# One bound register for 1323 indirect gathers, in place of one register move each

## The chip, the cores and the metric

The kernel runs on one core of a Trainium2 chip, as one launch. The metric is the device time of a run in microseconds (us); the table below gives the median of three runs. The profile shown is of one further execution, taken by the hardware profiler.

## The reference

Two relational graph attention layers over a graph of 3125 nodes with 768 features and 53125 edges, then a residual and a layer norm. The edges come sorted by destination; each has one of three relations. Cut to what matters:

```
def rgat_conv(x, W, q, k, b, src, dst, etype, heads, out_ch, n_nodes):
    xr = einsum('nd,rdf->rnf', x, W)          # 3 x 3125 rows of 768
    oi, oj = xr[etype, dst], xr[etype, src]   # gathered by edge
    alpha = leaky_relu(oi @ q + oj @ k, 0.2)
    m = segment_max(alpha, dst)
    e = exp(alpha - m[dst])
    z = segment_sum(e, dst)
    a = e / (z[dst] + 1e-16)
    msg = a[:, :, None] * oj.reshape(-1, heads, out_ch)
    return segment_sum(msg, dst) + b

h = elu(rgat_conv(x, W1, q1, k1, b1, ..., heads=4, out_ch=192))
h = rgat_conv(h, W2, q2, k2, b2, ..., heads=1, out_ch=768)
out = layernorm(x + h)
```

All arithmetic is in float32.

## The kernel before, in words

Nodes are taken in 25 blocks of 128. The edges of a block lie in slots of 128 edges: 18 slots for each of 24 blocks and 9 for the last, 441 slots in all (`SL`, `SLL`, `NK`). A layer makes a table in DRAM with one row for each node and relation, 9600 rows (`NP * R`), which holds the node's features times that relation's weights and the attention's product for the source side. For every slot, one indirect DMA on GpSimd's queue then gathers 128 rows of a table, one to each partition, by the 128 row numbers of the slot.

There are three stages, and each gathers every slot once:

- Stage 1 (`phase1`) makes layer 1's table `ftab1` by dense products on TensorE (line 626, evicted by ScalarE on line 638). Beside it, it gathers the small rows of `kt1` (4 numbers an edge) into the buffers `kt`, and from them works out the softmax weights `pall` of layer 1 (`a_alpha`, line 560, is the first that reads the gathered numbers).
- Stage 2 (`phase2`) walks the slots: it gathers a row of 772 numbers an edge from `ftab1` into nine buffers `share`, splits each into a high and a low part (ScalarE line 785, VectorE line 799), makes a one-hot matrix `sel` of the destinations (line 787, on VectorE for every third slot and on GpSimd for the others), and adds the slot up with TensorE (line 818). Between them stand the dense products that make layer 2's table `ftab2` (line 873).
- Stage 3 (`phase3`) gathers rows of `ftab2` into six buffers `G` of six slots each, takes the softmax (line 1017 first reads the gathered numbers), adds the slots up (line 1090), and writes the layer norm's output.

The order of the instructions on each engine is written out by hand: a loop over slots (or over dense products in stage 1) calls the parts of the work at fixed distances, under `manual_schedule`. GpSimd runs its instructions in that order: in stages 1 and 3 nearly only gathers, in stage 2 gathers with the one-hot matrices of two slots in three between them. A gather may wait for a buffer to come free, and for an earlier gather's landing: eight semaphores (`DMASW0` to `DMASW7`) are used by the gathers in turn.

All gathers go through one helper, `gather_rows`. It passes `bounds_check=NP * R - 1`, the highest row that may be read. Row numbers of places past a block's own edges are set beyond it, so nothing is read for them; for four blocks, which are the first to fill their buffers, the row numbers are cut to the highest row (`rfirst`), so that every place is filled. The instruction takes the bound from a register of GpSimd. Given a plain number, it is lowered to two instructions: a register move, which stands right before the gather in GpSimd's program, and the gather.

A second kernel for edges that are not sorted as assumed stands behind a test at the end, and isn't executed with these inputs.

Of the kernel before, what the change touches and what calls it, by code (L numbers as in the profile page):

```python
# [18 lines left out]
DRAM = bass.MemoryType.DRAM  # L19
# [5 lines left out]
#: Masks an edge out of a maximum: a power of two, exact in bfloat16.  # L25
BIG = float(2**100)
#: Past every row of a layer's sums.
NOWHERE = 1 << 13
#: Slots per load of the destination rows.
# [7 lines left out]
#: Slots of 128 edges that a block of 128 nodes has on the fast path.  # L37
SL = 18
CAP = SL * P
#: And the last block, of fewer nodes.  # L40
SLL = 9
#: Entries before and behind the edges in their copies in DRAM.
FRONT = 256
BACK = CAP + 256
#: Rows gathered at once in the second layer, in slots.
PART = 6
#: Of so many slots there, those whose sums are float32 products.
# [4 lines left out]
def kernel(  # L52
# [9 lines left out]
    """The same for edges sorted by destination: at most CAP to a block of 128 nodes, 128 to a node.  # L62

    Returns a number that isn't 0 where the edges aren't so, and `out` then isn't to be used; every
    address stays in bounds for any edges.

    A block's edges start at `S[b]`, in SL slots of 128, and what is past its own edges counts for
    nothing. Rows come with (p * row) split into H + L, H of float32r's precision, so that two
    passes of one-hot matmuls add them up exactly as float32 would; dense products are HH + HL + LH.
    """  # L70
# [20 lines left out]
    OOB = float(1 << 20)  # L91

# [32 lines left out]
    def split3(to, q, work, shape):  # L125
        """q as a sum of three bfloat16."""
        c = work.tile(shape, F32, name="c3", bufs=2)
        V.tensor_copy(to[0], q)
        V.tensor_sub(c, q, to[0])
        V.tensor_copy(to[1], c)  # L130
        c2 = work.tile(shape, F32, name="c3", bufs=2)
        V.tensor_sub(c2, c, to[1])
        V.tensor_copy(to[2], c2)

    class Buffers:
        """What is loaded at first, in its order, each as soon as a buffer is free."""
# [32 lines left out]
    # ------------------------------------------------------------------ edges  # L169
    def prepare(work, bank, wide, half):  # L170
        """Copies of the edges' arrays for the slots, where the blocks start, and the flag; bit by bit."""
# [50 lines left out]
        # what is out of order, and nodes of more than 128 edges  # L222
# [26 lines left out]
    def transposes(psum, blocks):  # L249
        """The blocks turned, side by side: DT / 2 tiles of two parts."""  # L250
        pts = []
        for i in range(DT // 2):
            pt = psum.tile([P, 2, 2 * P], F32, name=f"pt{i}", bufs=2)
            for f in range(2):
                for c, a in enumerate(blocks):
                    T.transpose(pt[:, f, c * P:(c + 1) * P], a[:, (2 * i + f) * P:(2 * i + f + 1) * P], ident)
            pts.append(pt)
        return pts

    def split_parts(work, pts, w, name="t"):  # L260
        """The first w columns of each as H + L."""
        parts = []
        for i, pt in enumerate(pts):
            H, L = (work.tile([P, 2, w if name != "t" else 2 * P], F32R, name=f"{name}{s}{i}",
                              bufs=2 if name == "t" else 1) for s in "HL")
            S.copy(H[:, :, :w], pt[:, :, :w])
            V.tensor_sub(L[:, :, :w], pt[:, :, :w], H[:, :, :w].bitcast(F32))
            parts.append((H, L))
        return parts

    def times(to, a, parts):
        """a's products with what was split, added up."""
# [8 lines left out]
    # ------------------------------------------------------------------ attention of layer 1, early  # L281
    def weights_kq(buf, work, psum, bank, wk, kqs, wH, wL, nodes, more):
        """W1 split; W1[r] @ [k | q] split, and to the left of it zeros."""
# [53 lines left out]
    def nodes_kq(buf, pre, work, psum, bank, wk, kqs, wH, wL, qq, more, edges_ready):  # L337
        """The k products of all nodes, to DRAM, and the q; between them block 0's products with W1."""
        NCH = NB // 2 + 1

        def chunk(m):
            """Its first block, how many: at first block 0 alone."""
            return (2 * m - 1, min(2, NB + 1 - 2 * m)) if m else (0, 1)
# [37 lines left out]
        def first(i):  # L381
            """A third of a product of block 0 and half of W1[r]."""
# [31 lines left out]
        def begin(m):  # L414
            """Beside the weights' products: the first nodes."""
# [4 lines left out]
        # how many of block 0's thirds go beside which step  # L420
# [20 lines left out]
    def gather_rows(to, tab, b, j):  # L441
        """Past a block's edges nothing is read; a buffer's first rows are read whole."""
        i = ridx[:, b]
        if b in first_rows:
            i = rfirst[:, first_rows[b]]
        G.indirect_dma_start(out=to, out_offset=None, in_=tab, in_offset=_index(i[:, j:j + 1]),  # L446
                             bounds_check=NP * R - 1, oob_is_err=False)
# [6 lines left out]
    def at(t, rw, off, ap, s):  # L454
        """A view of an edge array in DRAM from edge s + off on."""
# [25 lines left out]
    def second_weights(r, wH, wL):  # L481
        """W2[r] in W1[r]'s place, with W2[r] @ [k | q] between its halves; piece by piece."""
# [9 lines left out]
    # ------------------------------------------------------------------ layer 1's tables and weights  # L492
    def phase1(pre, work, psum, wH, wL, qq):
# [103 lines left out]
        # buffers that are free by then  # L597
# [95 lines left out]
        # the last blocks' products go by W1[r], that W2[r] can take its place  # L693
# [4 lines left out]
        # what is done beside which product, by block  # L698
# [4 lines left out]
        for b in [*reversed(range(NB - 1)), NB - 1]:  # L703
            for d, f in steps if b < NB - 1 else last:
                # the first blocks' gathers are behind
# [35 lines left out]
    # ------------------------------------------------------------------ layer 1's sums, layer 2's table  # L741
    def phase2(work, psum, wH, wL):
# [11 lines left out]
        # the last block, of fewer slots, comes first  # L754
# [3 lines left out]
        def slot(k):  # L758
            """Block and slot of it."""
# [8 lines left out]
        def whole(k):  # L768
            """Of the first slots, with no dense products yet, every other's sums are float32 products."""
            return k < 8 and k % 2 == 1  # L770
# [92 lines left out]
        def d_part(b, r, c, i):  # L863
            """A third of a product of a block of h and half of W2[r]."""
# [70 lines left out]
    def x_load3(b):  # L935
        """x and layer 2's bias of a block, for the third phase."""
        nc.sync.dma_start(xbs[b % len(xbs)], xb_d[b * P:(b + 1) * P, :])

    # ------------------------------------------------------------------ layer 2's sums, residual, layer norm
    def phase3(work, psum):  # L940
# [24 lines left out]
        def a_local(b):  # L965
            """The slots' destinations, by slot; past 256 not exact, and none of the block's."""
# [5 lines left out]
        def a_spread(b, i):  # L972
            """Four slots' destinations to all partitions."""
# [76 lines left out]
        def whole(k):  # L1050
            """Slots whose sums are float32 products, to spare the split of their rows."""
            return k % 3 == 0 if late(k) else k * WHOLE[0] % WHOLE[1] < WHOLE[0]

        def late(k):
            """After the last gather."""
# [109 lines left out]
    with tc.manual_schedule():  # L1165
        with tc.tile_pool(name="share", bufs=1) as pool:
            share = [pool.tile([P, RW], F32, name=f"share{i}") for i in range(9)]
            # in the third phase: x and layer 2's bias, then the output
            two = pall.rearrange("p b j h -> p (b j h)")
            xbs = [t[:, :D] for t in share] + [two[:, i * D:(i + 1) * D] for i in range(2)]  # L1170
            with tc.tile_pool(name="wbuf", bufs=1) as wbuf:
                wH = wbuf.tile([P, R * DT, D + 2], F32R, name="wH")
                wL = wbuf.tile([P, R * DT, D + 2], F32R, name="wL")
                with tc.tile_pool(name="pre", bufs=1) as pre:
                    qq = pre.tile([P, NB, H1, R], F32, name="qq")
                    with tc.tile_pool(name="work0", bufs=1) as work, tc.tile_pool(
                        name="psum0", bufs=1, space=PSUM
                    ) as psum:
                        # products in one half, what they are turned into in the other
# [31 lines left out]
def kernel(  # L1211
# [9 lines left out]
    """Two relational graph attention layers, x + layers, layer norm.  # L1221

    Edges are first sorted by block of 128 destinations into slots of 128 edges, each slot of one
    block (`count_edges`, `place_edges`). A layer then makes a table of x @ W[r] with the attention's two products
    (`dense`), and walks the slots: it gathers the edges' rows, and keeps a running softmax of
    each block's 128 nodes (`edges`), as flash attention does, so that the destinations' degrees
    are free.
    """
# [11 lines left out]
    # A block of c edges has max(1, ceil(c / 128)) slots.  # L1240
# [43 lines left out]
    def attention_weights(ly, w, kq, work, psum):  # L1284
        """W[r] @ k behind the first half of W[r]'s columns, W[r] @ q behind the second."""
# [15 lines left out]
    def table_rows(ly, work):  # L1301
        """Buffers for rows of the table: per head its features and a one, then the heads' k products."""
# [7 lines left out]
    def dense(ly, block, w, rows, tab, qtab, work, psum, before=None):  # L1310
        """The table's rows and the q products of every node, block by block of nodes."""
# [42 lines left out]
    def count_edges(prep):  # L1354
        """What a slot needs of each edge (rows of the two tables, place in the block), and its rank."""
# [19 lines left out]
        # rank of each edge among its block's: first along a partition, then over partitions  # L1375
# [19 lines left out]
    def place_edges(prep, psum, erec, oh, s, cnt, below, ones):  # L1395
        """Edges to their slots; what is left of a slot leads nowhere."""
# [4 lines left out]
        # slots of each block, and the first of them  # L1401
# [10 lines left out]
        # an edge's place, in rows of rec_d: slot by slot within a partition  # L1412
# [23 lines left out]
        # a slot's block, and whether it is its block's first or last  # L1436
# [16 lines left out]
        # where a slot's block goes once it is whole; else nowhere  # L1453
# [22 lines left out]
    def edges(ly, tab, qtab, agg, work, psum):  # L1476
        """Each block's weighted sums of rows, and of the weights, by head: each slot adds its own to
        those so far, scaled to the maxima so far."""
# [21 lines left out]
        def scores(k):  # L1500
# [4 lines left out]
            # one where edge e leads to node n, by node and by edge; a penalty where it doesn't  # L1505
# [98 lines left out]
    def per_node(ly, n, a, plus, work):  # L1604
        """What a block's sums give: over the sum of the weights, plus `plus`."""
# [139 lines left out]
```

## Time and profile before

| | |
|---|---|
| median of 3 runs | 2310.36 us (2303.12 to 2312.99) |
| span of the profiled execution, first to last instruction | 2301.8 us |
| instructions in the span | 37988 |
| TensorE busy | 2053.6 us, 89% |
| TensorE weight loads busy | 1779.3 us, 77% |
| VectorE busy | 1636.5 us, 71% |
| ScalarE busy | 1232.2 us, 54% |
| GpSimd busy | 1751.5 us, 76%, 1684 instructions |
| gathers (line 446) | 1323, mean 1069 ns (`kt`), 1136 ns (`share`), 1161 ns (`G`) |
| register moves of line 446 | 1323, 29 ns each |
| moved by the DMA engines | 507.92 MB |

The profiled execution has no separate device time beside its span; the median of the runs is 8.6 us above the span.

How to read it: PE is TensorE, PEld its weight loads, DVE VectorE, ACT ScalarE, POOL GpSimd, SP the engine that issues most plain DMAs. A name with a q (POOLq) is the engine's sequencer, [...] its time is not counted as busy. [...] "out<-in" names the buffers, L446 is line 446, x378 a count. In a list of waits, the number triple is the total in us, how often, and the longest one; in brackets in a list in order of time stands how long the engine was idle before. "issue" is time in which the engine waited for nothing that the profile shows.

### The profile page before, as it was taken

What the parts mean: (1) busy time and instruction counts of PE and PEld (TensorE: products, weight loads), DVE (VectorE), ACT (ScalarE), POOL (GpSimd) and SP (SyncE); (2) the same over time, 40 slices, a digit from 0 to 9 for tenths busy, and PEclk for the clock granted to TensorE, in tenths of its full rate; (3) what the DMA queues carried; (4) which work ended last, traced back from release to release, by engine and by line L of the source; (5) the groups of instructions that cost most, each with busy time, mean ns of one, the idle gap of its engine ahead of it and who ended that gap; (6) DMA issues with size and microseconds to landing.
All of it is one profiled execution on the core that took longest, in us unless ns stands there. A gap on an engine that the chain in (4) does not pass through costs nothing.

```text
span 2301.8 us, 37988 instructions
## 1 busy us (share of the span) xinstructions
PE 2053.6 (89%) x11380; PEld 1779.3 (77%) x11380; DVE 1636.5 (71%) x4349; ACT 1232.2 (54%) x2745; POOL 1751.5 (76%) x1684
## 2 busy tenths in 40 slices
PE   6999988888985899999999999999499898898986
PEld 5888877888885899999999999998365555555554
DVE  7634434444433899999999999995387777777766
ACT  5411211111111788888888888884255554555553
POOL 4157777777776888888888888883777777777773
PEclk9989999999998899999999999999699999999998
DMA  6545444454455977777777777775888888888882
GB/s 181 171 135 177 163 150 143 161 168 145 158 193 168 316 243 230 233 228 240 235 231 237 236 235 234 234 230 186 292 287 285 284 293 278 289 261 285 274 268 73
DMA packets 153482, 507.92 MB, mean 221 GB/s; under 512 B 40362, under 2 KB 53697, under 8 KB 153269
## 3 DMA queue, kind: packets, MB, share of 16 engines
q0 software_dynamic: 85408, 333.97, 48.0%
q1 hardware_dynamic: 57631, 155.46, 18.8%
q10 hardware_dynamic: 10230, 15.98, 2.1%
q8 instruction: 94, 1.54, 0.3%
q14 instruction: 119, 0.97, 0.1%
HBM read 428.29 MB, written 93.81 MB: 227 GB/s over the span
## 4 chain that ended last, share of the span: by engine, by line
PE 39%; DMA 8%; POOL 8%; DVE 6%; issue 6%; ACT 2%; POOLq 0%; DVEq 0%; ACTq 0%
PE po L873 14%; PE acc L1090 13%; PE acc L818 10%; DMA G<-ftab,ridx 5%; POOL share L446 3%; POOL sel L787 2%; POOL G L446 2%; DVE L L799 2%; DVE L L1079 1%; DMA share<-ftab,ridx 1%; ACT H L785 1%; PE bc L978 1%; DMA G<-ftab,rfirst 1%; DMA share<-ftab,rfirst 1%; PE pt L848 1%
## 5 line engine op out<-in xcount | busy, mean ns | idle before, releaser
L785 ACT ACTIVATE H<-share,pall 128x193 fp32r<-128x193 f32 x1748 | 643.9, 447 | 104.2 <-DMA share<-ftab,ridx 46.0
L799 DVE SCALAR_TENSOR_TENSOR L<-share,pall,H 128x193 fp32r<-128x193 f32 x1748 | 648.0, 437 | 25.8 <-ACT H L785 15.7
L873 PE MATMUL po<-wH,hT 128*128 128x386 f32 (+1 forms) x1800 | 533.2, 339 | 0.0
L446 POOL DMA_INDIRECT G<-ftab,ridx x378 | 438.7, 1161 | 115.2 <-issue 55.8
L446 POOL DMA_INDIRECT kt<-kt,ridx x378 | 404.2, 1069 | 115.2 <-issue 113.0
L446 POOL DMA_INDIRECT share<-ftab,ridx x378 | 429.6, 1136 | 81.4 <-DVE L L799 41.9
L626 PE MATMUL po<-wH,xT 128*128 128x384 f32 x1584 | 444.3, 353 | 0.7 <-ACT xT L612 0.7
L1090 PE MATMUL acc<-G,selp 128*128 128x386 f32 x904 | 360.1, 524 | 1.0 <-DVE selp L1064 1.0
L873 PEld LDWEIGHTS po<-wH,hT 128*128 128x128 f32 x1800 | 334.6, 189 | 0.6 <-DVE hT L861 0.5
L873 PE MATMUL po<-wL,hT 128*128 128x386 f32 (+1 forms) x900 | 305.0, 339 | 0.0
L626 PEld LDWEIGHTS po<-wH,xT 128*128 128x128 f32 x1584 | 301.6, 196 | 3.4 <-issue 0.8
L626 PE MATMUL po<-wL,xT 128*128 128x384 f32 x792 | 275.2, 348 | 0.0
L818 PE MATMUL acc<-H,sel 128*128 128x386 f32 x874 | 241.8, 358 | 20.1 <-POOL sel L787 10.3
L638 ACT COPY share<-po 128x384 f32<-128x384 f32 x144 | 69.0, 479 | 326.4 <-PE po L626 259.7
L787 POOL TENSOR_SCALAR sel<-frow,fdl 128x128 fp32r<-128x128 f32 x291 | 224.9, 773 | 13.2 <-PE acc L818 1.3
L1090 PEld LDWEIGHTS acc<-G,selp 128*128 128x128 f32 x904 | 171.9, 201 | 79.0 <-issue 12.0
L1079 DVE SCALAR_TENSOR_TENSOR L<-G,p,H 128x772 fp32r<-128x772 f32 x215 | 217.5, 1013 | 21.2 <-ACT H L1068 20.2
L818 PE MATMUL acc<-L,sel 128*128 128x386 f32 x874 | 226.6, 341 | 0.0
L1068 ACT ACTIVATE H<-G,p 128x772 fp32r<-128x772 f32 x215 | 194.9, 934 | 41.8 <-issue 33.8
L818 PEld LDWEIGHTS acc<-H,sel 128*128 128x128 f32 x874 | 149.7, 189 | 54.4 <-POOL sel L787 45.4
L560 DVE TENSOR_TENSOR a<-qe,kt 128x72 f32<-128x72 f32 x25 | 5.8, 234 | 239.8 <-DMA kt<-kt,ridx 203.2
L873 PEld LDWEIGHTS po<-wL,hT 128*128 128x128 f32 x900 | 169.8, 189 | 0.0
(230 smaller groups left out, 2933.6 us busy)
## 6 DMA issues: line engine op xcount, KB each, us to landing
ftab<-r SPq DMA_DIRECT2D x75, 386.0 KB
ftab<-share SPq DMA_DIRECT2D x72, 386.0 KB
sT<-dr_d SPq DMA_DIRECT2D x25, 576.0 KB
share<-in_L_gnn_W_dram SPq DMA_DIRECT2D x36, 384.0 KB
w_d<-w2hl SPq DMA_DIRECT2D x18, 768.0 KB
share<-in_x_dram SPq DMA_DIRECT2D x25, 384.0 KB
xb_d<-share SPq DMA_DIRECT2D x25, 384.0 KB
xr<-in_x_dram SPq DMA_DIRECT2D x23, 384.0 KB
```

The lines of the kernel that those rows point to most:

```text
L446: G.indirect_dma_start(out=to, out_offset=None, in_=tab, in_offset=_index(i[:, j:j + 1]), bounds_check=NP * R - 1, oob_is_err=False)
L626: T.matmul(po[:, :HALF], xT[:, s, t, :], w[:, i, sl], start=(n == 0), stop=(n == 3 * DT - 1))
L638: S.copy(to, po[:, :HALF].rearrange("p (h f) -> p h f", h=2))
L785: S.activation(H[:, c], g[:, c], AF.Copy, scale=pall[:, b, j, h:h + 1])
L787: (V if k % 3 == 0 else G).tensor_scalar(sel, row, dl[:, b, j:j + 1], None, op0=ALU.is_equal)
L799: V.scalar_tensor_tensor(L[:, c], g[:, c], pall[:, b, j, h:h + 1], H[:, c].bitcast(F32), op0=ALU.mult, op1=ALU.subtract)
L818: T.matmul(acc[:, c, :HW], sel, a[:, c * HW:(c + 1) * HW], start=(j == 0 and i == 0), stop=(k in ends2 and i == 1), skip_group_check=True)
L848: T.transpose(pt[:, t // 3, (t % 3) * P:(t % 3 + 1) * P], s["ey"][:, t * P:(t + 1) * P], ident)
L873: T.matmul(po[:, :wd], hT[:, k, t, :], w[:, r * DT + t, sl], start=(t == 0 and n == 0), stop=(t == DT - 1 and n == 2))
L1068: S.activation(H, g, AF.Copy, scale=p)
L1079: V.scalar_tensor_tensor(L, g, blk[b]["p"][:, j:j + 1], st[k][1].bitcast(F32), op0=ALU.mult, op1=ALU.subtract)
L1090: T.matmul(acc[:, c, :HW], sel, a[:, c * HW:(c + 1) * HW], start=(j == 0 and i == 0), stop=(k in ends and i == len(parts) - 1))
```

## The change

The bound is put in a register once, at the head of the fast kernel, and the gathers name the register:

```
@@ tile_rgat2_sorted_kernel
     V, S, G, T = nc.vector, nc.scalar, nc.gpsimd, nc.tensor
     OOB = float(1 << 20)

+    top = G.to_reg(NP * R - 1)
+
     dram = ctx.enter_context(tc.tile_pool(name="fdram", bufs=1, space=DRAM))
...
@@ gather_rows
         G.indirect_dma_start(out=to, out_offset=None, in_=tab, in_offset=_index(i[:, j:j + 1]),
-                             bounds_check=NP * R - 1, oob_is_err=False)
+                             bounds_check=top, oob_is_err=False)
```

Comments are removed from the file as well, which leaves the lines where they were but for the two that are added: line 446 is line 448 after the change. In the lowered program the one move stands ahead of the first gather.

More of the change, by code (lines that the diff above doesn't have):

```diff
@@ L91 @@
     OOB = float(1 << 20)
+    top = G.to_reg(NP * R - 1)
     dram = ctx.enter_context(tc.tile_pool(name="fdram", bufs=1, space=DRAM))
@@ L446, in gather_rows @@
         G.indirect_dma_start(out=to, out_offset=None, in_=tab, in_offset=_index(i[:, j:j + 1]),
-                             bounds_check=NP * R - 1, oob_is_err=False)
+                             bounds_check=top, oob_is_err=False)
     def start(b, into):
```

## The prediction

> **What bounds the kernel now.** I read the stages first, then GpSimd's waits, then the two rows that the change touches.
>
> The kernel runs in three stages of 441 gathers each (24 blocks of 18 slots, one of 9). The busy time of the engines over them, columns: stretch, its length, busy us of each engine with instruction counts, TensorE's clock, share of the DMA engines, GB/s:
>
> ```profile
> 105.00:735.00 630.00, 548.38 (x3397) 524.67 (x3395) 260.86 (x579) 113.93 (x226) 469.34 (x444) 0.94 0.49 158
> 735.00:1600.00 865.00, 836.74 (x4601) 799.55 (x4602) 804.71 (x2345) 725.19 (x1949) 724.29 (x732) 0.98 0.77 238
> 1600.00:2302.00 702.00, 587.48 (x2800) 379.85 (x2798) 492.24 (x1228) 339.72 (x463) 522.16 (x453) 0.91 0.80 261
> ```
>
> TensorE (first number) is the fullest engine everywhere. GpSimd (last one) looks loose at 74 to 84%, but its waits say otherwise:
>
> ```profile
> POOL kt L446 <- issue: 131.6, 432, 0.3
> POOL G L446 <- issue: 70.7, 232, 0.3
> POOL share L446 <- DVE L L799: 47.9, 242, 0.3
> ```
>
> The last number is the longest single wait. For gathers it is 0.3 us whatever "releaser" is named: this is no waiting but a fixed pause between two gathers. Taken one by one from the trace's instruction list, the 440 pauses between gathers in stage 1 have a median of 0.305 us and a maximum of 0.32; the 440 in stage 3 a median of 0.305 and a maximum of 0.31. So in stages 1 and 3 GpSimd is full: a gather of 1.0 us and more, 0.3 us, the next gather. In stage 3 441 gathers take 510 us and their pauses 134, which is 644 of the 702, and the vector engine waits 105 us for their rows (DVE a L1017 on G, 22 times). **A shorter pause would therefore be worth time**; whether the removed instruction is in the pause is the whole question.
>
> **What is removed** is GpSimd's register move before each gather, the second row here (duration min/median/max in ns, first and last start):
>
> ```profile
> L446 POOLq MOVE  x1323: 29/29/29, 105.5 to 2243.8; - x189
> L446 POOL DMA_INDIRECT G<-ftab,ridx x378: 1005/1012/2377, 1686.2 to 2238.8; - x189
> L446 POOL DMA_INDIRECT G<-ftab,rfirst x63: 1005/1009/2072, 1610.1 to 2253.0; - x63
> ```
>
> (It stands first.) "POOLq" is GpSimd's sequencer, not its data path. The last move is at 2243.8, the last gather starts at 2253.0: the move came 9.2 us, some seven gathers, early. The same at the beginning:
>
> ```profile
> L446 POOLq MOVE  x11: 29/29/29, 105.5 to 134.1; - x11
> L446 POOL DMA_INDIRECT kt<-kt,rfirst x6: 997/1056/1155, 128.0 to 134.8; - x6
> ```
>
> When the sixth gather starts, eleven moves are done. Over all 1323 gathers, pairing the n-th move with the n-th gather, the move is at least 1.03 us ahead of its gather's start (in stage 2, at 776.9), and by the median 8.9, 6.7 and 7.4 us in the three stages.
>
> Two pauses side by side settle most of it. In 1203.7 to 1206.7 the sequencer executes no move at all; at 1802.87, inside the pause that ends at 1802.93, it does:
>
> ```profile
> 1205.47 1.20 POOL L446 DMA_INDIRECT share<-ftab,ridx  x1 [0.30 <-DVE L L799]
> ...
> 1802.93 1.01 POOL L446 DMA_INDIRECT G<-ftab,ridx  x1 [0.30 <-DVE sel L1070]
> ```
>
> Both pauses (in brackets) are 0.30 us. Sorting all pauses by how long before its end the last move ran (under 0.1 us up to over 1.6 us) gives a median of 0.304 or 0.305 us in every class and stage.
>
> [...] moves for later gathers run during a gather. [...] never more than 7 extra moves are done when a gather starts. [...] a stage 3 gather is longer the more of its first 0.99 us the vector engine is busy (correlation 0.72); I use this for a rival.
>
> **The change, part by part.**
> 1. *Removed:* 1322 moves net. The instruction lists of both programs show 2207 register moves on GpSimd before and 885 after (884 belong to the branch that isn't executed here, or to other lines), and no other difference of kind, order, wait or buffer on any engine. On the sequencer that is 1322 x 0.029 = 38.3 us; with the step from a move to what follows it (0.075 us, 1201.019 to 1201.094 in the list) 1322 x 0.075 = 99 us. On the path: 0. [...] the sequencer is 1.03 us ahead or more, and needs 0.075. Without that cover it would cost 38 to 99 us.
> 2. *Where the cover is thinnest:* at four gather starts (three in stage 2, one in stage 3) no later move was done yet. Their own moves were still over 1 us early. At most 4 x 0.075 = 0.3 us comes of it.
> 3. *Added:* one move ahead of the first gather, 0.03 us, in a stretch where that gather waits 21.4 us for ACT xT L612. Nothing.
> 4. *The gather itself* still names a register. The trace has no gather whose register was written long before, so I bound it: no less than -0.029 us each (the move cannot take more than itself out of the pause) and, since nothing excludes a loss, +0.029. I take 0, by the pause at 1205.47, which no move is near. The ends are -38 and +38 us.
> 5. *What is queued behind:* the sequencer's next obstacle is the same as before, [...] so it only waits there 0.03 to 0.075 us longer. Nobody waits for it. No DMA is added or moved, on SP's queue or GpSimd's. Instruction fetch shrinks: 2.51 MB on the page's two instruction queues for 37988 instructions is 66 bytes each, so 87 KB of 507.92 MB. Nothing.
>
> Sum: 0, at most -0.3 us, against the profiled span of 2301.8. The median of the runs shown is 2310.36, 8.6 above the span, with 2303.12 as the lowest; I keep that distance and predict **2310 us**.
>
> **Rivals.**
> *A. The pause holds the move after all* (faster). For it: stages 1 and 3 have no slack on GpSimd, so any part of the pause that goes is felt. 0.029 us from each of 441 pauses is 12.8 us a stage; stage 3, where the chain of waits runs through gathers, gives 12.8 (2297), all three 38.3 (2272). Against it: the pause does not change with the move's place, and after a TENSOR_SCALAR it is 0.171 us although that gather has its move too. Chance 0.12, most of it in 2285 to 2298.
>
> *B. Gathers stretch* (slower). The gathers of the three stages take 31, 60 and 67 us more than if each had its stage's minimum, 157 us together, and the correlation above ties this to vector work. If gathers fall differently against it, the stretch can grow. 7.3% more of it, 11.5 us, is where it decides; at 10% more, 15.7 us, the time is 2326. Against it: a queued gather starts when the last one is done, so its place does not depend on the sequencer's pace. Chance 0.06.
>
> *C. The change isn't carried out*, and every gather still gets a move: 2310, the same time. The instruction list speaks against it; its chance is inside "same".
>
> **How the numbers follow.** A measurement of this kernel tells from no change about 0.5%, 11.5 us: the runs shown span 2303 to 2313. No change (with C) 0.82, its own range 2300 to 2320; A 0.12; B 0.06. The range takes in run-to-run spread on both sides and the near end of A, one stage's 12.8 us: 2297 to 2320. The ends of step 4 are left to A and B, as their chances allow.
>
> **What would show it right or wrong.** Right: the move's row falls from 1323 to 1, the page's instructions from 37988 to about 36666, the pause between gathers stays at 0.305 us (0.17 after a TENSOR_SCALAR), the gathers' minimum at 0.99 to 1.0 us, the waits DVE a L560 and L1017 near 240 and 139 us. Step 1 is wrong if the longest and the usual wait in front of gathers fall to 0.27 us or less; step 4 if the gathers' own minimum moves; B if the minimum and the pause stay and only the mean of G's gathers rises from 1.16 us. The whole prediction is wrong if the median leaves 2297 to 2320.

## The result, and the profile after

Nothing that can be measured changed. Twelve runs of each kernel, taken together: after 2308.27 us median (2302.34 to 2313.53), before 2304.71 (2300.62 to 2315.73); the ratio is 1.0002, 95% interval 0.9987 to 1.0018 (the quotient of the two medians, 1.0015, lies inside it). Runs that took over 1.5% more than the fastest of their kernel, 13 of 39 of the kernel before and 3 of 20 of one without bounds in a session of the experiments, are left out here and below. The profiled execution of after has a span of 2311.7 us against 2301.8, which is no more than single runs of one kernel differ by, and means nothing by itself.

The page counts 36666 instructions, 1322 fewer. The move is there once; the first line is the row of the new line 93, the others are the gathers of stage 3, now line 448 (duration min/median/max in ns, first and last start in us). Rows of POOLq, GpSimd's sequencer, are register moves, semaphore waits (EVENT_SEMAPHORE), branches and drains; the gathers are rows of POOL. In the trace of before 726 of the 1323 moves start while an earlier gather runs.

```profile
L93 POOLq MOVE  x1: 29/29/29, 108.3 to 108.3; - x1
...
L448 POOL DMA_INDIRECT G<-ftab,ridx x378: 1005/1012/2377, 1690.8 to 2249.3; - x189
...
L448 POOL DMA_INDIRECT G<-ftab,rfirst x63: 1005/1009/2069, 1615.9 to 2263.1; - x63
```

In both rows the gather's shortest and median durations are those of before to the nanosecond. GpSimd's waits (total us, times, longest):

```profile
POOL kt L448 <- issue: 132.2, 434, 0.3
POOL G L448 <- issue: 72.5, 238, 0.3
POOL share L448 <- DVE L L801: 47.1, 238, 0.3
```

The pause is still there, 0.3 us, neither longer nor shorter. Taken one by one, it has a median of 0.305 us between gathers in all three stages, and 0.171 after a TENSOR_SCALAR (the making of a one-hot matrix), with no move in front of any gather. In order of time, a stretch of stage 3 (start, duration, and in brackets the idle time before):

```profile
1808.95 1.01 POOL L448 DMA_INDIRECT G<-ftab,ridx  x1 [0.30 <-PE pq L1002]
1810.27 1.13 POOL L448 DMA_INDIRECT G<-ftab,ridx  x1 [0.30 <-DMA G<-ftab,ridx]
1811.70 1.20 POOL L448 DMA_INDIRECT G<-ftab,ridx  x1 [0.30 <-PE acc L1092]
```

### The profile page after: what moved, and what is told of

Same layout as the page of the kernel before. It is cut to its first block, busy times and chain, and to the rows that moved or that the text cites. A ratio compares the mean times of both kernels' runs of the same rounds, so it can differ in the third digit from the quotient of the medians.

```text
span 2311.7 us, 36666 instructions
## 1 busy us (share of the span) xinstructions
PE 2057.0 (89%) x11380; PEld 1781.9 (77%) x11380; DVE 1638.3 (71%) x4349; ACT 1231.7 (53%) x2745; POOL 1759.5 (76%) x1684
## 2 busy tenths in 40 slices
DMA packets 153473, 507.84 MB, mean 220 GB/s; under 512 B 40363, under 2 KB 53698, under 8 KB 153270
## 3 DMA queue, kind: packets, MB, share of 16 engines
q0 software_dynamic: 85408, 333.97, 47.8%
## 4 chain that ended last, share of the span: by engine, by line
PE 43%; DMA 7%; POOL 7%; DVE 6%; issue 4%; ACT 1%; DVEq 0%; POOLq 0%; ACTq 0%
PE po L875 15%; PE acc L1092 14%; PE acc L820 12%; DMA G<-ftab,ridx 5%; POOL share L448 3%; POOL sel L789 2%; POOL G L448 2%; DVE L L1081 1%; DVE L L801 1%; ACT H L787 1%; DMA share<-ftab,rfirst 1%; PE bc L980 1%; PE pt L850 1%; DMA G<-ftab,rfirst 1%; PE pq L1002 0%
## 5 line engine op out<-in xcount | busy, mean ns | idle before, releaser
L448 POOL DMA_INDIRECT G<-ftab,ridx x378 | 444.6, 1176 | 115.2 <-issue 57.3
L1081 DVE SCALAR_TENSOR_TENSOR L<-G,p,H 128x772 fp32r<-128x772 f32 x215 | 217.5, 1012 | 20.0 <-ACT H L1070 19.0
L562 DVE TENSOR_TENSOR a<-qe,kt 128x72 f32<-128x72 f32 x25 | 5.9, 234 | 238.0 <-DMA kt<-kt,ridx 193.3
```

The source lines that it names most:

```text
L1081: V.scalar_tensor_tensor(L, g, blk[b]["p"][:, j:j + 1], st[k][1].bitcast(F32), op0=ALU.mult, op1=ALU.subtract)
```

## The experiments

They ask three things. Does a move cost the sequencer anything, and how many can it hide? What happens when its lead is taken away? And would a shorter pause, or a shorter gather, have been felt? All are edits of the kernel after. Each ratio is against runs of the kernel before in the same session: it took 2510 us in the first session (8, 24 and 48 moves, and the first run without bounds) and 2309 to 2310 us in the other two. In the first session stage 1 ran longer: with 8 moves it took 734 us from the start of its first gather to that of its last, against 601 in the profile of before, and TensorE's clock there was 0.85 against 0.94.

### 8, 12, 18, 24 and 48 more moves before each gather

The moves write registers that nothing reads. For 12 and 18 the same with six registers, twice and three times; for 24 and 48 with eight, three and six times.

```
+    idle = [G.alloc_register(f"idle{n}") for n in range(8)]
...
+        for _ in range(1):
+            for r in idle:
+                G.reg_mov(r, NP * R - 1)
+            G.keepalive_nop([G.lower_val_access(r) for r in idle])
         G.indirect_dma_start(out=to, out_offset=None, in_=tab, in_offset=_index(i[:, j:j + 1]),
                              bounds_check=top, oob_is_err=False)
```

With 8, expected:

> After, with 8 register moves that nobody reads put in front of every gather (10584 more in all). Theory (the sequencer runs ahead of the gathers, and a move costs it 0.029 to 0.075 us): 8 x 0.075 = 0.6 us fit into a gather's 1.3 us, so the time is that of after, within 0.5%, and the pause between gathers stays 0.305 us. Rival A (moves lie in the pause): 8 x 0.029 us x 1323 = 307 us more, 2615 us, and the pause grows to 0.54 us.

Measured: 2500.5 us, ratio 0.9976 (0.9947 to 1.0006). The pause's median stayed 0.305 us in all stages. 10,584 moves more cost nothing that these runs can tell. In that session single gathers of stage 1 waited for other engines, up to 11.6 us, and a small cost there could have been hidden by that; the run with 12 moves below has no such waits.

With 24:

> After, with 24 unread register moves in front of every gather. Theory: at 0.075 us a move, 1.8 us and the sequencer's other work exceed a gather's 1.3 us, [...] the sequencer sets the pace: over 500 us more, and gathers no longer start 0.305 us after the last one but irregularly; at 0.029 us a move, 0.7 us still fit and nothing changes. Rival A: 24 x 0.029 x 1323 = 921 us more.

Measured: 2921.2 us, ratio 1.160 (1.153 to 1.167): the sequencer sets the pace. These are some 410 us more, not over 500: a move costs less than the 0.075 us of the expectation. With 48:

> After, with 48 unread register moves in front of every gather. Theory: the sequencer sets the pace at either price; the difference to 24 moves, divided by 24 x 1323, is what one move costs the sequencer, 0.029 to 0.075 us (921 to 2381 us between the two if 24 is already beyond the threshold). Rival A: 921 us between the two, and the same slope from 8 to 24.

Measured: 4790.9 us. The difference to 24 is 1869.7 us, over 24 x 1323 moves 0.0589 us each. In both traces one move follows the other after 0.0575 us, of which the profile shows 0.029 as the move. Subtracting 24 x 0.0575 from the median step from gather to gather (1.840 us in stage 1, 1.907 in stage 3; 1.302 and 1.316 in the trace of before) leaves 0.46 and 0.53 us for the rest of what the sequencer does for a gather; with 48 it leaves 0.49 and 0.53. This model, an estimate from two traces, was put to the test with 12 and 18:

> After, with 12 unread register moves in front of every gather. The runs with 24 and 48 give a model of the sequencer: 0.0575 us a move and 0.46 us (stage 1) or 0.53 us (stage 3) for the rest of a gather. With 12 that is 1.15 and 1.22 us, less than the 1.30 to 1.32 us from gather to gather: all moves are hidden, 2300 to 2320 us, median pause 0.305. Rival A: 12 x 0.029 x 1323 = 460 us more.

> The same with 18. By the model 1.495 us (stage 1) and 1.56 us (stage 3) from gather to gather as the median, more than 1.30 to 1.32: [...] the pauses are no longer 0.305, and the time rises by 110 to 190 us; stage 2, where gathers are 1.88 us apart, keeps its length. Rival A: 690 us more.

Measured with 12: 2311.1 us, ratio 1.0006 (0.9991 to 1.002). With 18: 2470.5 us, ratio 1.069 (1.066 to 1.072), 161 us more; the steps' medians are 1.492 and 1.558 us, against 1.495 and 1.56 foretold, and stage 2 kept its length (835 us from its first to its last gather, against 828). The same moment of stage 1, first with 12 moves, then with 18:

```profile
402.70 1.00 POOL L453 DMA_INDIRECT kt<-kt,ridx  x1 [0.30 <-issue]
404.00 1.01 POOL L453 DMA_INDIRECT kt<-kt,ridx  x1 [0.30 <-issue]
```

```profile
402.45 0.99 POOL L453 DMA_INDIRECT kt<-kt,ridx  x1 [0.50 <-issue]
403.94 1.00 POOL L453 DMA_INDIRECT kt<-kt,ridx  x1 [0.50 <-issue]
```

The pause between gathers has a median of 0.305 us with no move in front of a gather, with one and with 8, and is 0.30 us in the list with 12. With 18 it is 0.50 us: the model's step of 18 x 0.0575 + 0.46 = 1.495 us, less 0.99 us of gather. By the model, which is an estimate, (1.302 - 0.46) / 0.0575 = 14.6 moves fit under a gather of stage 1; 12 did and 18 didn't. The kernel before had one.

### The lead taken away

A drain stands in front of each gather. In the run with the register a drain on the sequencer lasts 4.138 us by the median (0.997 to 7.072), and a gather lands 3.9 us after its issue by the median (2.1 to 6.8). Two kernels differ only in the bound's form:

```
+        G.drain()
         G.indirect_dma_start(out=to, out_offset=None, in_=tab, in_offset=_index(i[:, j:j + 1]),
                              bounds_check=top, oob_is_err=False)             # with the register
                              bounds_check=NP * R - 1, oob_is_err=False)      # with a move
```

> After, with a drain of GpSimd in front of every gather: its sequencer stands until all that GpSimd issued is done, so that it can't run ahead. Much slower, by what a gather's landing takes: the sequencer, which was 7 gathers ahead, now has one at a time, 3 to 6 us each, 4000 to 8000 us in all. It is the partner of the next run.

> The same drains, with the bound given as a number, so that a register move stands between each drain and its gather. Theory (the lead of the sequencer is what hides the move): with the lead gone the moves are on the path, and this is slower than its partner by 1323 x 0.0575 = 76 us (0.0575 us is the step from move to move in the runs with 24 and 48). Rival A (a fixed part of the pause, 0.029 us): 38 us. Rival N (a move costs nothing even without the lead): no difference.

Measured: 6003.5 us (5999.7 to 6010.2) with the register, 6067.8 (6061.5 to 6072.5) with the moves. The difference is 64 us, 0.049 us a gather; by the extremes of the runs, 51 to 73 us. It is more than A's 38 and below the 76 of the theory; why it is less than 0.0575 us a gather isn't shown. From gather to gather the medians rise by 0.048, 0.055 and 0.058 us in the three stages (from 3.16, 4.83 and 4.74 us). One drain against the gather before it: the gather, with the register, starts at 2003.30 and is done on GpSimd after 1.01 us, its rows land at 2007.08, and the drain ends at 2007.15. So the very edit that does nothing here is worth 64 us where the sequencer has no lead. The row of the moves in the second kernel, and of the drains in the first:

```profile
L449 POOLq MOVE  x1323: 29/29/29, 114.6 to 6021.9; - x189
```

```profile
L448 POOLq DRAIN  x1323: 997/4138/7072, 106.3 to 5944.8; - x189
```

The last move starts at 6021.9; the last gather of that trace starts at 6022.7, 0.8 us later. In the kernel before, these two were 9.2 us apart.

### A longer pause, stage by stage

Two small memsets on GpSimd stand in front of each gather of one stage:

```
+    fill = keep.tile([P, 64], F32, name="fill")
...
+        if tab is kt1:            # stage 1; tab1: stage 2; tab2: stage 3
+            for _ in range(2):
+                G.memset(fill, 0.0)
```

> After, with two memsets of 128x64 on GpSimd in front of each of the 441 gathers of stage 1; by the fixed pauses before and after a small operation the pause between gathers grows from 0.305 to some 0.5 to 0.6 us. Theory of the prediction (GpSimd is full in stage 1, a change of its pause is felt): 441 x 0.2 to 0.3, 90 to 130 us more. Rival (TensorE sets stage 1, the gathers only keep up): under 20 us more.

> Two memsets of 128x64 in front of each gather of stage 2. In stage 1 such a pair added 0.25 us to a gather and 107 us to the time, in stage 3, where the sequencer's waits fell between, 0.6 us and 268 us. If GpSimd paces stage 2 as well, 100 to 270 us more; if TensorE or the vector engine does (837 and 805 of 865 us busy), under 50 us more.

> The same two memsets in front of each gather of stage 3. Theory (stage 3's chain runs through the gathers): 90 to 130 us more. Rival (TensorE or the DMA engines set stage 3): under 20 us more.

Measured:

| memsets in | time, us | more than before | stage's length, first to last gather |
|---|---|---|---|
| stage 1 | 2416.1, ratio 1.047 (1.043 to 1.051) | 107 | 710 against 601: +109 |
| stage 2 | 2600.0, ratio 1.125 (1.122 to 1.128) | 290 | 1117 against 828: +289 |
| stage 3 | 2577.9, ratio 1.118 (1.113 to 1.122) | 268 | 911 against 643: +268 |

Each stage grows by what the pauses on GpSimd grow by, and the time grows with it: no slack of another engine takes it up. The trace of before shows the same of stage 2, where the prediction saw a loose GpSimd, 84% busy. Its rows on GpSimd there (busy us, mean ns, and idle us in front):

```profile
L446 POOL DMA_INDIRECT share<-ftab,ridx x378 | 429.6, 1136 | 81.4 <-DVE L L799 41.9
L446 POOL DMA_INDIRECT share<-ftab,rfirst x63 | 69.8, 1108 | 23.8 <-ACT e L583 9.6 <-DVE L L799 6.0 <-issue 4.0
L787 POOL TENSOR_SCALAR sel<-frow,fdl 128x128 fp32r<-128x128 f32 x291 | 224.9, 773 | 13.2 <-PE acc L818 1.3
```

From the start of the first gather to the end of the last are 829 us: 499 of gathers, 222 of one-hot matrices between them, and 108 of pauses. Once the stage has begun, no pause in front of a gather is longer than 0.306 us, or 0.176 after a TENSOR_SCALAR. So GpSimd is full in stage 2 too: the fixed pauses are the rest.

Stage 1's 107 us lie in the 90 to 130 expected. The expectation for stage 3 missed the size, 268 us where 90 to 130 were expected: the pause grew by 0.62 us and not by 0.2 to 0.3. The one for stage 2 left both sides open; the side with under 50 us is refuted, and the 290 us lie above the 100 to 270 of the other. The two lists show why; first stage 1's memsets, then stage 3's:

```profile
403.53 1.00 POOL L452 DMA_INDIRECT kt<-kt,ridx  x1
404.53 0.38 POOL L451 MEMSET fill<- 128x64 f32 x2
405.06 1.55 POOL L452 DMA_INDIRECT kt<-kt,ridx  x1
```

```profile
1900.39 0.37 POOL L451 MEMSET fill<- 128x64 f32 x2
1901.32 1.01 POOL L452 DMA_INDIRECT G<-ftab,ridx  x1 [0.56 <-DVE L L1085]
```

In stage 1 the gather starts 0.15 us after the memsets (405.06 - 404.53 - 0.38), in stage 3 0.56 us after them. In stages 2 and 3 most gathers (434 and 406 of 441 in the trace of before, 25 in stage 1) have a wait on the semaphore of an earlier gather's landing that is an instruction of the sequencer (EVENT_SEMAPHORE). For the gather at 1901.32 it runs at 1900.60, just as the second memset starts: the sequencer's lead is gone there, and stage 2's trace shows the same 0.56 us behind its memsets. What took the lead isn't shown. So the rows of stages 2 and 3 carry more than a longer pause; what a shorter gather is worth in these stages is shown by the next kernel.

### No bound at all

```
@@ where the row numbers are made
-            if b in first_rows:
-                V.tensor_scalar(rfirst[:, first_rows[b], :], ridx[:, b, :], NP * R - 1, None, op0=ALU.min)
+            V.tensor_scalar(ridx[:, b, :], ridx[:, b, :], NP * R - 1, None, op0=ALU.min)
@@ gather_rows
-        if b in first_rows:
-            i = rfirst[:, first_rows[b]]
-        G.indirect_dma_start(out=to, out_offset=None, in_=tab, in_offset=_index(i[:, j:j + 1]),
-                             bounds_check=top, oob_is_err=False)
+        G.indirect_dma_start(out=to, out_offset=None, in_=tab, in_offset=_index(i[:, j:j + 1]))
```

Places past a block's own edges now read the last row instead of nothing; they count for nothing in the sums, as before.

> After, without any bound: all row numbers are cut to the highest row on VectorE (one more small operation a block instead of four in all), and the gathers name no register. All 128 rows of every slot are then read, 6% more rows than edges. Theory: a gather doesn't pay for its register, the pause stays 0.305 us and the shortest gather 0.99 us; the time is that of after, or up to 1% more where the added rows fill the DMA engines. Rival (the register operand is what costs, whenever it is written): the pause or the shortest gather falls by 0.029 us or more, and the time by 13 to 38 us.

Measured in the first session: 2508.9 us, ratio 0.9971 (0.9944 to 0.9999). The pause stayed at 0.305, but the shortest gather of stage 1 fell to 0.945 us. The theory's sentence that a gather doesn't pay for its bound is wrong, and of the rival the part on the gather came true, the 13 to 38 us less did not. The same kernel once more:

> The kernel without bounds once more, on another chip: on the first its shortest gather was 0.047 us shorter than with a bound (0.945 against 0.992), but TensorE's clock of 0.83 in stage 1 there made TensorE the bound of that stage. Where the clock in stage 1 is near 0.94, gathers pace stages 1 and 3 (shown by the added memsets), and 441 x 0.047 = 21 us a stage should be felt: 20 to 50 us less, 2260 to 2290. Rival (the 6% more rows that are read eat it, or the gain of the first chip was chance): 2300 to 2330.

Measured: 2252.3 us (2248.1 to 2262.7), ratio 0.9757 (0.9727 to 0.9787): 57 us less, more than the 20 to 50 expected, which counted two stages of three. The rows of the gathers:

```profile
L446 POOL DMA_INDIRECT kt<-kt,ridx x441: 944/952/1719, 130.9 to 712.9; - x147
L446 POOL DMA_INDIRECT share<-ftab,ridx x441: 943/1019/1784, 723.5 to 1521.9; - x147
L446 POOL DMA_INDIRECT G<-ftab,ridx x441: 952/959/2327, 1568.2 to 2201.6; - x147
```

The medians are 0.045, 0.07 and 0.053 us below the 997, 1089 and 1012 ns that the kernel after has. It is the bound that costs, not the skipped rows: the `rfirst` gathers with a bound read all rows too, and take as long as the others (medians 997, 1087 and 1009 ns in the kernel after). Whether the time goes into the comparison or into reading the register that the gather names is open; no run has one without the other. From first to last gather the stages lost 19, 29 and 10 us against the profile of before, 58 together; what lies outside the stages took 7 back, so that the two profiled executions differ by 51. Stage 1's loss is 441 times the fall of its mean gather, 0.044 us. So is stage 3's with 0.021: its longer gathers became longer, which took back more than half of the 0.053. In stage 2 the means give 441 x 0.091 = 40 us, of which the one-hot matrices took back 14 (their mean rose from 773 to 821 ns, x291).

Why was nothing of it seen in the first session? By one profiled execution each, stages 2 and 3 had gained there too: 801 and 673 us from first to last gather, where the run with 8 moves of that session took 832 and 684. Stage 1 was longer instead, 782 us against 734, and its gathers waited for others:

```profile
POOL kt L446 <- DVE rel L519: 210.0, 22, 23.3
```

So a shorter gather of stage 1 could hardly be felt there. That TensorE was the bound of that stage, as the expectation says, isn't shown: its clock was 0.83, against 0.96 in the later session, but it was busy for 610 of 820 us. Both sessions were on a chip of the same number, so it was not another chip. What made stage 1 so long is open.

## Why the prediction was right, point by point

**The number.** The mechanism held: the sequencer's lead hides the moves, which cost 64 us where the drains take the lead away. That 2310 lies within 2 us of the measured 2308.27 is chance, for single runs of one kernel spread over 11 to 15 us, and the median of before went from 2310.36 in three runs to 2304.71 in twelve. The 8.6 us between span and median, which I kept, were that spread: in each run of the kernel after, the device time is 1.8 us above the span.

**What bounds the kernel.** "In stages 1 and 3 GpSimd is full" held: what the memsets added there came out in full. It said too little of stage 2, which I left out for its busy share of 84%, with the vector engine and TensorE busier. With its fixed pauses GpSimd is full there as well, and the stage grows with GpSimd's work in the run with memsets and shrinks with it in the one without bounds. Here that did no harm, since nothing was taken from GpSimd's own work.

**Step 1, the moves are off the path,** held: removing one, or adding 8 or 12, gives the same time. The size of the step was off. I took 0.075 us from a move to what follows it, which is a step from a move to a semaphore wait; it is 0.0575 from move to move. The uncovered price of "38 to 99 us" was measured as 64 with the drains, and would be 76 by the step. Both say that the 29 ns of the profile's row are only a half to 60% of what a move takes, so the ends of step 4, and what rival A asked for, were priced too low.

**Steps 2 and 3,** at most 0.3 us and nothing, are too small to be seen; no run tells them from zero.

**Step 4, the gather that names an old register,** held: the pause is unchanged to the nanosecond, and so are the shortest and median gather of stages 1 and 3. What I didn't ask there is what the bound itself costs. That was the larger term all along: 0.045 to 0.07 us of every gather, on the engine that sets the pace. The change kept it.

**Step 5** held: the waits DVE a L562 and L1019 are 238 and 143 us, against 240 and 139, and the DMA engines moved 507.84 MB, against 507.92.

**Rival A** (the pause holds the move) is refuted by 8 and 12 moves, where it asked for 307 and 460 us. **Rival B** (gathers stretch) didn't come: the mean of G's gathers in the `ridx` row rose from 1161 to 1176 ns, 441 times which is 7 us of the profiled execution, and over all runs the interval of the ratio leaves 4 us at most. Its ground was also weaker than the prediction says. From the trace of before, the correlation of a stage 3 gather's duration with the vector engine's busy time in its first 0.99 us comes out at 0.39 over the 441 gathers, not 0.72. Over the gather's whole duration it is 0.75, but that is no evidence: a longer gather meets more vector work by being longer. That vector work makes a gather longer isn't shown by any run here. **Rival C** is excluded by the row with one move; the sequencer's register moves in the two traces are 1324 and 2.

## What to carry to other kernels

Here register moves on the sequencer cost nothing that could be measured as long as the sequencer was ahead (ratio 1.0006 with 12 in front of each gather), and 0.049 us each where it wasn't (the drains). To know that of another kernel, compare the start of the n-th such instruction with the start of the n-th operation that it belongs to, and see whether the pause in front of the operation changes with it. Before taking work from a full engine's program, ask which of it that engine's data path executes; here the move was the sequencer's and free, and the bound inside the gather was the engine's and worth 57 us. Add a known amount of work on one engine, stage by stage, to learn where a saving on it would be felt: busy shares (97% for TensorE, 84% for GpSimd) called stage 2 TensorE's, but GpSimd's work and its fixed pauses filled it.

## What the runs showed of the hardware that was not expected

- A register move takes GpSimd's sequencer 0.0575 us, twice its row in the profile; 12 of them in front of each gather hide where gathers are 1.3 us apart (ratio 1.0006), 18 don't (1.069).
- A bound makes a gather of 128 rows longer by 0.045 us (16-byte rows of `kt`) to 0.07 us (rows of 772 numbers in stage 2; 0.053 in stage 3), whether or not rows are skipped.
- Reading 16.8 MB more (350.78 against 333.97 MB on GpSimd's DMA queue) while dropping the bound still gained 2.4%.
- GpSimd was full at a busy share of 84%: fixed pauses, 0.305 us between two gathers and 0.171 us after a TENSOR_SCALAR, took the rest.
